# A graph network on one core: the last product taken in node order, and one-hot matrices and comparisons moved into one ring of seven buffers

## The chip, the cores and the metric

The kernel runs on one core of a Trainium2 chip. The time is device microseconds of one launch, the median of several runs: 3683.91 us over 12 runs, from 3669.29 to 3695.47.

The core has five engines, each with an instruction order of its own: PE multiplies matrices (PEld is its loading of weights), DVE (VectorE) and ACT (ScalarE) work on elements, POOL (GpSimd) issues here the gathers, and SP issues DMAs. They meet through semaphores.

## The reference

There are 16 graphs of N = 1024 nodes with C = 64 channels and a weighted adjacency matrix of 1024 x 1024 for each. Four layers follow one another, each of the form x = layernorm(x + f(x, adj)):

```
layer 0   f = adj @ (x @ W) + b
layer 1   neighbours with every second one or so removed ("dilated"), then per node and channel
          a weighted sum of three quantiles over the neighbours that are left, then an MLP
layer 2   h = x @ W_embed; three times h = relu(adj @ (h @ Wl + bl)); f = h @ W_proj + b_proj
layer 3   t = adj @ x; f = where(t > 0.5, 1, 0)
```

The last of them is the product that the change is about: t[node, channel] = sum over m of adj[node, m] * x[m, channel], compared with 0.5, added to x and normalised over the 64 channels of a node.

## The kernel before, in words

A graph is kept as T = 8 tiles of P = 128 nodes. Its adjacency is transposed once and stands in SBUF as `adjT[p, t, m, n]` (float32): the weight of the edge from node m * 128 + p to node t * 128 + n.

For each graph b three long pieces of work and some short ones are written as Python generators that emit a few instructions and yield a duration:

- `words_of` (L559): loads the adjacency row by row, transposes it on PE, compares it with zero on DVE into `nb` (L582 and L583, 1024 float16 per partition), packs the bits by a product with powers of two (L594), computes layer 0 and stores the transposed adjacency in DRAM (L590).
- `front` with `listing` (L613, L647): sorts the nodes by degree. DVE builds eight one-hot matrices `perm` (L717, one for each tile of 128 nodes), PE multiplies each with the packed words (L722 and L723, 16 instructions for each one), ACT copies the result out (L759 and L760), and DVE extracts from it the lists of neighbours (L768 to L793). A second one-hot, `back_to` (L621), is used once.
- `gathered`, `masked`, `quantiles`, `summed`: POOL gathers the neighbours' rows (L921), ACT masks them (L976), DVE sorts them by a network of minimum and maximum (L1026), ACT and PE sum the weighted rows (L1062, L1055).
- `back` (L1253): the rest of layer 1, layer 2 and layer 3. It begins in `to_nodes` (L1086), which brings the sums back from degree order to node order: the sums are split into three bfloat16 `pieces` (L1092); then for s = 0 to 7 ACT makes a one-hot `ones_at` in two instructions (L1105 and L1106) and PE multiplies it with the pieces (six instructions, L1110). It ends with layer 3: `aggregate` (L426) takes x3 as the weights of PE and streams the adjacency, 512 columns at a time, so that the product comes out as channels by nodes; ACT copies the two halves out of PSUM (L434); eight transposes (L1350) bring it into node order; DVE compares, adds (L1353) and normalises.

A float32 matmul stands in the trace as two records, each with a weight load of its own, so the 16 matmuls of L431 are 32 records.

The order of the instructions on every engine is fixed when the program is built. A heap holds the generators by a planned time; the earliest emits its next instructions and is put back later by what it yielded, times a stretch (178/181 for `back`, L1384). Planned time per graph is 192.06 units (`LENGTHS`); the `back` of a graph, the `front` of the next one and the `words_of` of the one after that run at the same time, with the quantiles of the groups between. So the eight `perm` and the eight `ones_at` fall into the same stretch. An engine runs what was emitted for it strictly in that order, so one instruction that waits holds up all that was emitted after it. Each gather on POOL is made to wait for the fifth last DVE and the fourth last ACT instruction emitted before it (`follow`, L899).

Buffers rotate by tag: the n-th allocation of a tag takes slot n modulo the number of slots, and who writes first into a slot waits until the readers of what stood there are done. Before, `nb`, `perm` (with `back_to`) and `ones_at` have a tag and two slots each. So `perm` number t waits until PE has read `perm` number t - 2, and `ones_at` number s until PE has read number s - 2.

The lines in `general` (L1151 on) are a fallback for graphs that do not fit the fixed sizes; no instruction of it stands in the trace.

Of the kernel before, what the change touches and what calls it, by code (L numbers as in the profile page):

```python
# [11 lines left out]
F16 = mybir.dt.float16  # L12
BF16 = mybir.dt.bfloat16
# [7 lines left out]
P = 128  # L21
# [185 lines left out]
def kernel(  # L207
# [36 lines left out]
    tmp = ctx.enter_context(tc.tile_pool(name="tmp", bufs=2))  # L244
# [7 lines left out]
    ident = const.tile([P, P], F32, name="ident")  # L252
# [170 lines left out]
            nc.scalar.copy(dst[:, h * HALF:(h + 1) * HALF], pt[:C, :])  # L423
            yield 1.0

    def aggregate(dst, adjT, src, bank):  # L426

        for h in range(NH):
            pa = bank()
            for m in range(T):  # L430
                nc.tensor.matmul(pa[:C, :], src[:, m, :], adjT[:, h * TH:(h + 1) * TH, m, :],  # L431
                                 start=(m == 0), stop=(m == T - 1))
                yield 1.3
            nc.scalar.copy(dst[:, h * HALF:(h + 1) * HALF], pa[:C, :])  # L434
            yield 0.7

    def layernorm(u, y, who, mean=False):

        def col(name):
# [119 lines left out]
    def words_of(st):  # L559


        b = st["b"]
        while b >= LIVES and "done" not in state[b - LIVES]:
            yield 0.5
        st["mb"] = mask_of(b)
        xt = load_x(b)
        hi = his[b % 2]
        lo = act.tile([P, T, W + 2], F16, tag="lo", name="lo", bufs=2)
        l0 = Layer0(xt)
        if b == 0:  # L570

            st["adjT"] = adjT = big.tile([P, T, T, P], F32, tag="adjB", name="adjB")
        else:
            st["adjd"] = adjd = dram.tile([P, T, T, P], F32, tag="adjd", name="adjd", bufs=LIVES)

        def block(t):
            if b == 0:
                return adjT[:, t]
            return big.tile([P, T, P], F32, tag="adjF", name="at", bufs=3)

        def words(t, a, at):
            nb = tmp.tile([P, T, P], F16, tag="nb", name="nb")  # L582
            vector.tensor_scalar(nb, at, 0.0, None, op0=ALU.is_gt)  # L583
            yield 0.3
            vector.tensor_tensor(nb[:, t, :], nb[:, t, :], off_diag, ALU.mult)
            if b:
                while "x1 is there" not in state[b - 1]:
                    yield 0.5
                yield from l0.feed(t, at)
                nc.scalar.dma_start(adjd[:, t], at)  # L590
            pw = psum_tp()
            for c in range(T):
                half = c // TH
                nc.tensor.matmul(pw[:, half * (W + 1):(half + 1) * (W + 1)], nb[:, c, :],  # L594
                                 pow2[:, c, :], start=(c % TH == 0), stop=(c % TH == TH - 1))
            yield 0.7
            nc.scalar.copy(hi[:, t, :W], pw[:, :W])
            nc.scalar.copy(lo[:, t, :], pw[:, W:2 * W + 2])
            yield 0.6

        yield from transposed(b, block, words)
        xc = act.tile([P, T, R], F32, tag="xc", name="xc", bufs=LIVES)
        st["x1"] = xc[:, :, :C]
        st["words"] = hi, lo, xc
        if b == 0:
            while "permuted" not in st:
                yield 0.5
            for t in range(T):
                yield from l0.feed(t, adjT[:, t])
        yield from l0.end(st["x1"])  # L610
        st["x1 is there"] = True

    def front(st):  # L613
        b = st["b"]
        while "words" not in st or (b >= 2 and ("all in", len(GROUPS) - 1) not in state[b - 2]):
            yield 0.5
        hi, lo, xc = st["words"]
        yield from listing(st, hi, lo)

        part, tile_of = st["home"]  # L620
        back_to = tmp.tile([P, T, P], F16, tag="perm", name="back_to")  # L621
        vector.tensor_tensor(back_to, iota[:, :P].unsqueeze(1).to_broadcast([P, T, P]),
                                spread(part, P), ALU.is_equal)
        yield 0.8
        in_tile = small.tile([P, T, T], F16, tag="in_tile", name="in_tile", bufs=1)
        vector.tensor_tensor(in_tile, iota[:, :T].unsqueeze(1).to_broadcast([P, T, T]),
                                spread(tile_of, T), ALU.is_equal)
        yield 0.6
        gone = small.tile([P, T, T, 2], F16, tag="gone8", name="gone8", bufs=1)
        vector.tensor_tensor(gone, in_tile.unsqueeze(3).to_broadcast([P, T, T, 2]),  # L630
                                st["gone"].unsqueeze(2).to_broadcast([P, T, T, 2]), ALU.mult)
# [12 lines left out]
        nc.scalar.dma_start(table[1:N + 1, :].rearrange("(t p) c -> p t c", p=P), xc)  # L644
        yield 3.0

    def listing(st, hi, lo):  # L647
# [5 lines left out]
        deg, do, h, odd = col("deg"), col("do"), col("h", I32), col("odd")  # L653
# [72 lines left out]
        if st["b"] == 0:  # L726

            rooms = [srt.tile([P, TH, N], F16, tag="x", name="perms", bufs=4) for _ in range(NH)]
            perms = [rooms[t // TH][:, t % TH, :] for t in range(T)]
            for t in range(T):  # L730
                one_hot(t, perms[t])
                yield 0.5
            halves = [range(h * TH, (h + 1) * TH) for h in range(NH)]
        else:
            for t in range(T):
                perm = tmp.tile([P, N], F16, tag="perm", name="perm")
                one_hot(t, perm)
# [348 lines left out]
    def to_nodes(dst, st):  # L1086
# [10 lines left out]
        st["moved"] = True  # L1097
        banks = [psum_mm() for _ in range(NH)]
        for s in range(T):
            ones_at = tmp.tile([P, N], BF16, tag="ones_at", name="ones_at", bufs=2)  # L1100
            if st["b"] == B - 1 and s % 3:
                vector.tensor_scalar(ones_at, iota, st["minus"][:, s:s + 1], 0.0,
                                        op0=ALU.add, op1=ALU.is_equal)
            else:
                nc.scalar.activation(ones_at, iota, AF.Abs, bias=st["minus"][:, s:s + 1])  # L1105
                nc.scalar.activation(ones_at, ones_at, AF.Relu, bias=1.0, scale=-1.0)  # L1106
            yield 1.9
            for h, bank in enumerate(banks):
                for i in range(S):
                    nc.tensor.matmul(bank[:C, :], pieces[:, i, s, :],  # L1110
                                     ones_at[:, h * HALF:(h + 1) * HALF],
                                     start=(s == 0 and i == 0), stop=False)
            yield 1.7
# [37 lines left out]
    def general(b):  # L1151
# [10 lines left out]
        def positions(t, a, at):  # L1162
            def col(name, dt=F32):
                return small.tile([P, 1], dt, tag="g" + name, name=name)

            nb = tmp.tile([P, N], F16, tag="nb", name="nb")
            vector.tensor_scalar(nb, a, 0.0, None, op0=ALU.is_gt)
            dg = nb[:, t * P:(t + 1) * P]
            vector.tensor_tensor(dg, dg, off_diag, ALU.mult)
            cum = tmp.tile([P, N], F16, tag="perm", name="cum")  # L1170
# [31 lines left out]
        nc.sync.dma_start(xrow, xT)  # L1202
        st["agg"] = act.tile([P, T, C], F32, tag="x3", name="agg")
        with tc.For_i(0, T, 1) as t:
            nb = tmp.tile([P, N], F16, tag="nb", name="nb")
# [3 lines left out]
            eT = tmp.tile([P, T, P], F16, tag="perm", name="eT")  # L1209
# [43 lines left out]
    def back(st):  # L1253
# [7 lines left out]
        adjT = st["adjT"]  # L1261
# [25 lines left out]
        def chan(name):  # L1287
            return act.tile([C, N], F32, tag="chan", name=name)
# [54 lines left out]
        x3 = node_tile("x3", "x3")  # L1343
        yield from residual(hT, wp_sb, 2 * C, x2, x3)

        tT = chan("tT")
        yield from aggregate(tT, adjT, x3, psum_mm)
        pt = psum_mm()
        for t in range(T):
            nc.tensor.transpose(pt[:, t * C:(t + 1) * C], tT[:, t * P:(t + 1) * P], ident[:C, :C])  # L1350
        yield 2.0
        u = wide_u("u3")
        vector.scalar_tensor_tensor(u, nodes(pt), 0.5, x3, op0=ALU.is_gt, op1=ALU.add)  # L1353
        yield 0.7
# [124 lines left out]
```

## Time and profile before

| | |
|---|---|
| median of 12 runs | 3683.91 us (3669.29 to 3695.47) |
| profiled execution, its own time | 3684.71 us |
| its span | 3682.8 us, so 1.9 us lie outside it |
| granted PE clock, mean | 0.814 |
| busy: PE, DVE, ACT, POOL | 72%, 76%, 52%, 59% |
| from the first `pieces` of one graph to that of the next | 216 us (596.1 to 3189.1 us holds twelve) |
| L431, the last product, PE | 264.4 us in 512 records |
| L1350, its transposes, PE | 16.7 us in 128 records |
| L434, its copies, ACT | 32 of about 0.578 us |
| L1105 and L1106, `ones_at` on ACT | 123 each, medians 1.134 and 1.057 us |
| L717, `perm` on DVE | 120, median 0.482 us |

No engine is busy all the time. In a program like this the sum of busy time says little; what counts in a stretch is the engine that the others wait for there, and the idle time that stands before an instruction on it. "remote" or "another core or an unknown queue" in an answer means that the instruction waited for a signal whose sender the profile cannot place. With one core there is no other core; it is in most cases a signal that came late.

### The profile page before, as it was taken

What the parts mean: (1) busy time and instruction counts of PE and PEld (TensorE: products, weight loads), DVE (VectorE), ACT (ScalarE), POOL (GpSimd) and SP (SyncE); (2) the same over time, 40 slices, a digit from 0 to 9 for tenths busy, and PEclk for the clock granted to TensorE, in tenths of its full rate; (3) what the DMA queues carried; (4) which work ended last, traced back from release to release, by engine and by line L of the source; (5) the groups of instructions that cost most, each with busy time, mean ns of one, the idle gap of its engine ahead of it and who ended that gap; (6) DMA issues with size and microseconds to landing.
All of it is one profiled execution on the core that took longest, in us unless ns stands there. A gap on an engine that the chain in (4) does not pass through costs nothing.

```text
span 3682.8 us, 49179 instructions
## 1 busy us (share of the span) xinstructions
PE 2665.1 (72%) x13765; PEld 1630.9 (44%) x13766; DVE 2797.7 (76%) x8020; ACT 1899.5 (52%) x6153; POOL 2171.0 (59%) x2078
## 2 busy tenths in 40 slices
PE   6334686867868686786868678686867868685678
PEld 5233453544445354454535444353544535342343
DVE  6287887968778796877879787786968778797650
ACT  2144555546464554646555564645556464555441
POOL 0666666566565656656665665656666665666600
PEclk8656797878879798887878888797888979777788
DMA  3232223323232332323233232323323232212110
GB/s 100 73 83 60 60 75 92 90 84 82 59 103 74 98 85 59 108 64 103 75 98 85 66 101 64 102 75 98 85 63 103 65 103 75 84 24 73 23 51 4
DMA packets 169079, 282.73 MB, mean 77 GB/s; under 512 B 99485, under 2 KB 102112, under 8 KB 166880
## 3 DMA queue, kind: packets, MB, share of 16 engines
q0 software_dynamic: 66048, 69.88, 11.6%
q1 hardware_dynamic: 67584, 142.01, 11.5%
q10 hardware_dynamic: 35168, 67.62, 4.9%
q8 instruction: 114, 1.87, 0.2%
q14 instruction: 165, 1.35, 0.1%
HBM read 204.33 MB, written 71.44 MB: 75 GB/s over the span
## 4 chain that ended last, share of the span: by engine, by line
DVE 32%; PE 31%; ACT 16%; another core or an unknown queue 14%; issue 5%; DMA 2%; DVEq 0%; ACTq 0%; POOL 0%; POOLq 0%
PE mm L1338 11%; DVE s L1026 8%; DVE g L1026 8%; ACT g L976 6%; PE ax L521 4%; DVE top L789 3%; PE mm L431 3%; ACT ones_at L1105 3%; PE mm L1110 2%; DVE cand L793 2%; ACT ones_at L1106 2%; ACT g L1062 2%; PE pa L1055 2%; PE tp L496 2%
## 5 line engine op out<-in xcount | busy, mean ns | idle before, releaser
L921 POOL DMA_INDIRECT g<-table,idx x1952 | 2048.0, 1049 | 1292.0 <-issue 336.7
L1338 PE MATMUL mm<-adjB,msg 128*128 128x512 f32 x1536 | 781.3, 631 | 41.6 <-issue 28.9
L1026 DVE TENSOR_TENSOR s<-g 128x384 f32<-128x384 f32 (+8 forms) x1200 | 576.3, 495 | 136.3 <-ACT g L976 94.9
L976 ACT ACTIVATE g<-g,bias 128x64 f32<-128x64 f32 (+9 forms) x2272 | 597.3, 339 | 87.3 <-DVE bias L972 71.7
L1026 DVE TENSOR_TENSOR g<-s 128x256 f32<-128x256 f32 (+10 forms) x1040 | 508.1, 500 | 8.8 <-remote 4.6
L1055 PE MATMUL pa<-g,ident 128*128 128x128 f32 (+1 forms) x1600 | 327.9, 333 | 132.4 <-ACT g L1062 80.4
L1062 ACT ACTIVATE g<-g,w 128x64 f32<-128x64 f32 x1552 | 393.0, 337 | 14.3 <-DVE w L1033 10.8
L1055 PEld LDWEIGHTS pa<-g,ident 128*128 128x128 f32 x1600 | 279.3, 230 | 269.9 <-issue 140.8
L1338 PEld LDWEIGHTS mm<-adjB,msg 128*128 128x128 f32 x1536 | 276.7, 200 | 263.8 <-issue 239.3
L1110 PE MATMUL mm<-ones_at,pieces 128*64 128x512 bf16 x768 | 246.0, 468 | 164.7 <-ACT ones_at L1106 128.0
L521 PE MATMUL ax<-at,xt 128*64 128x128 f32 x1920 | 306.1, 321 | 27.0 <-issue 26.6
L521 PEld LDWEIGHTS ax<-at,xt 128*64 128x64 f32 x1920 | 264.2, 164 | 90.0 <-issue 85.2
L431 PE MATMUL mm<-adjB,x 128*64 128x512 f32 x512 | 264.4, 647 | 14.6 <-issue 7.2
L1026 DVE TENSOR_TENSOR g<-g 128x256 f32<-128x256 f32 (+7 forms) x432 | 213.9, 505 | 4.4 <-remote 1.8
L1110 PEld LDWEIGHTS <-pieces 128*64 128x64 bf16 x768 | 95.4, 129 | 272.1 <-issue 229.3
L1026 DVE TENSOR_TENSOR g<-g,s 128x256 f32<-128x256 f32 (+5 forms) x512 | 209.1, 415 | 5.7 <-DVE at L674 1.3
L1341 ACT ACTIVATE hlT<-mm 128x512 f32<-128x512 f32 x96 | 57.3, 596 | 276.3 <-PE mm L1338 173.7
L722 PE MATMUL wd<-hi,perm 128*128 128x71 f16 x960 | 103.5, 223 | 126.6 <-DVE perm L717 94.6
L496 PE MATMUL tp<-ident,arow 128*128 128x128 f32 x1024 | 173.2, 300 | 29.6 <-DMA arow<-in_adj_dram 13.1
L1278 DVE TENSOR_TENSOR u<-mm,mb 128x512 f32<-128x512 f32 x32 | 22.1, 691 | 219.9 <-PE mm L1272 109.4
L498 ACT COPY at<-tp 128x512 f32<-128x512 f32 x240 | 138.0, 576 | 96.8 <-remote 55.1
L1105 ACT ACTIVATE ones_at<-iota,minus 128x1024 bf16<-128x1024 f16 x123 | 140.0, 1138 | 92.1 <-remote 47.2
(223 smaller groups left out, 4284.9 us busy)
## 6 DMA issues: line engine op xcount, KB each, us to landing
arow<-in_adj_dram SPq DMA_DIRECT2D x128, 512.0 KB
adjd<-at ACTq DMA_DIRECT2D x120, 512.0 KB
adjB<-adjd SPq DMA_DIRECT2D x15, 4096.0 KB
g<-table,idx POOLq DMA_INDIRECT x1952
table<-xc ACTq DMA_DIRECT2D x16, 264.0 KB
xt<-in_x_dram SPq DMA_DIRECT2D x16, 256.0 KB
out_dram<-y SPq DMA_DIRECT2D x16, 256.0 KB
stage<-table,packed POOLq DMA_INDIRECT x112
```

The lines of the kernel that those rows point to most:

```text
L431: nc.tensor.matmul(pa[:C, :], src[:, m, :], adjT[:, h * TH:(h + 1) * TH, m, :], start=(m == 0), stop=(m == T - 1))
L496: nc.tensor.transpose(pt[:, i * P:(i + 1) * P], a[:, j * P:(j + 1) * P], ident)
L498: nc.scalar.copy(at[:, h * TH:(h + 1) * TH, :], pt.rearrange("p (i n) -> p i n", n=P))
L521: nc.tensor.matmul(self.bank[:C, cols], self.xt[:, m + 1, :], at[:, m, :], start=(m == 0), stop=(m == T - 1))
L921: g = nc.gpsimd.indirect_dma_start(out=dst, out_offset=None, in_=st["table"], in_offset=bass.IndirectOffsetOnAxis(ap=index, axis=0))
L976: nc.scalar.activation(v, v, AF.Identity, bias=bias[:m, i, k:k + 1])
L1026: vector.tensor_tensor(box(bufs[mode >> 1 & 1], d, run, sd, count, tile), box(bufs[mode >> 3], a, run, sa, count, tile), box(bufs[mode >> ...
L1055: nc.tensor.matmul(pa[:, :(e - k) * nt * C], ident, rows_.rearrange("p (k c) -> p k c", c=R)[:, :, :C], start=(j == 0), stop=(j == len(run ...
L1062: nc.scalar.activation(slots(g, bufs[0], lo + r, lo + r + 1)[:, i, 0, :C], slots(g, bufs[at[r]], lo + r, lo + r + 1)[:, i, 0, :C], AF.Iden ...
L1105: nc.scalar.activation(ones_at, iota, AF.Abs, bias=st["minus"][:, s:s + 1])
L1110: nc.tensor.matmul(bank[:C, :], pieces[:, i, s, :], ones_at[:, h * HALF:(h + 1) * HALF], start=(s == 0 and i == 0), stop=False)
L1338: nc.tensor.matmul(pg, msg[:, m, :], adjT[:, h * TH:(h + 1) * TH, m, :], start=(m == 0), stop=(m == T - 1))
```

## The change

1. `aggregate`, its two copies and the eight transposes go. In their place, for each of the 8 node tiles, 8 matmuls take the 128 x 128 block `adjT[:, t, m, :]` as weights and stream the 64 columns of `x3[:, m, :]`, into 64 columns of one PSUM bank. The result is in node order at once. 64 matmuls (128 records with 128 weight loads) replace 16 (32 records) and the 8 transposes. They yield 1.4 after every four and 1.5 at the end: 23.9 planned units instead of 24.2.
2. `nb`, `back_to`, `perm` and `ones_at` share one tag, `onehot`, with seven slots of 2 KB per partition, instead of three tags with two slots each. In the fallback `nb`, `cum` and `eT` take the tag too.

```diff
-    def aggregate(dst, adjT, src, bank):
-
-        for h in range(NH):
-            pa = bank()
-            for m in range(T):
-                nc.tensor.matmul(pa[:C, :], src[:, m, :], adjT[:, h * TH:(h + 1) * TH, m, :],
-                                 start=(m == 0), stop=(m == T - 1))
-                yield 1.3
-            nc.scalar.copy(dst[:, h * HALF:(h + 1) * HALF], pa[:C, :])
-            yield 0.7
...
-            nb = tmp.tile([P, T, P], F16, tag="nb", name="nb")
+            nb = tmp.tile([P, T, P], F16, tag="onehot", name="nb", bufs=7)
...
-        back_to = tmp.tile([P, T, P], F16, tag="perm", name="back_to")
+        back_to = tmp.tile([P, T, P], F16, tag="onehot", name="back_to", bufs=7)
...
-                perm = tmp.tile([P, N], F16, tag="perm", name="perm")
+                perm = tmp.tile([P, N], F16, tag="onehot", name="perm", bufs=7)
...
-            ones_at = tmp.tile([P, N], BF16, tag="ones_at", name="ones_at", bufs=2)
+            ones_at = tmp.tile([P, N], BF16, tag="onehot", name="ones_at", bufs=7)
...
-        tT = chan("tT")
-        yield from aggregate(tT, adjT, x3, psum_mm)
         pt = psum_mm()
         for t in range(T):
-            nc.tensor.transpose(pt[:, t * C:(t + 1) * C], tT[:, t * P:(t + 1) * P], ident[:C, :C])
-        yield 2.0
+            for m in range(T):
+                nc.tensor.matmul(pt[:, t * C:(t + 1) * C], adjT[:, t, m, :], x3[:, m, :],
+                                 start=(m == 0), stop=(m == T - 1))
+                if m % 4 == 3:
+                    yield 1.4
+        yield 1.5
         u = wide_u("u3")
         vector.scalar_tensor_tensor(u, nodes(pt), 0.5, x3, op0=ALU.is_gt, op1=ALU.add)
```

More of the change, by code (lines that the diff above doesn't have):

```diff
@@ L1164, in col @@
                 return small.tile([P, 1], dt, tag="g" + name, name=name)
-            nb = tmp.tile([P, N], F16, tag="nb", name="nb")
+            nb = tmp.tile([P, N], F16, tag="onehot", name="nb", bufs=7)
             vector.tensor_scalar(nb, a, 0.0, None, op0=ALU.is_gt)
@@ L1169, in positions @@
             vector.tensor_tensor(dg, dg, off_diag, ALU.mult)
-            cum = tmp.tile([P, N], F16, tag="perm", name="cum")
+            cum = tmp.tile([P, N], F16, tag="onehot", name="cum", bufs=7)
             vector.tensor_tensor_scan(cum, nb, nb, 0.0, op0=ALU.add, op1=ALU.max)
@@ L1204, in general @@
         with tc.For_i(0, T, 1) as t:
-            nb = tmp.tile([P, N], F16, tag="nb", name="nb")
+            nb = tmp.tile([P, N], F16, tag="onehot", name="nb", bufs=7)
             nc.sync.dma_start(nb, keys[ds(t * P, P), :])
@@ L1208, in general @@
             nc.sync.dma_start(e, removed[ds(t * P, P), :])
-            eT = tmp.tile([P, T, P], F16, tag="perm", name="eT")
+            eT = tmp.tile([P, T, P], F16, tag="onehot", name="eT", bufs=7)
             nc.sync.dma_start(eT, removed[:, ds(t * P, P)].rearrange("(m p) n -> p m n", p=P))
```

## The prediction

> **What bounds the kernel now.** I read the page first: the busy shares and the chain that ended last. No engine is full, and the chain is spread over three of them, so the time is made of waits between engines and has to be read stage by stage.
>
> ```profile
> PE 2665.1 (72%) x13765; PEld 1630.9 (44%) x13766; DVE 2797.7 (76%) x8020; ACT 1899.5 (52%) x6153; POOL 2171.0 (59%) x2078
> ...
> DVE 32%; PE 31%; ACT 16%; another core or an unknown queue 14%; issue 5%; DMA 2%; DVEq 0%; ACTq 0%; POOL 0%; POOLq 0%
> ...
> L431 PE MATMUL mm<-adjB,x 128*64 128x512 f32 x512 | 264.4, 647 | 14.6 <-issue 7.2 <-DVE x L468 6.5 <-DMA stage<-table,packed 0.6
> L1110 PE MATMUL mm<-ones_at,pieces 128*64 128x512 bf16 x768 | 246.0, 468 | 164.7 <-ACT ones_at L1106 128.0 <-issue 36.5
> ```
>
> The reader is to see that PE waits 128 us for the one-hots of ACT, and that 14% of the chain is late signals.
>
> Second, the lines L1105 (`ones_at` on ACT) and L717 (`perm` on DVE): how long the engine sat idle ahead of them, and what ended it. The instructions need nothing of PE but a free buffer, so a release by PE's L1110 or L723 is the wait for a slot. "remote" I count as the same wait with a late signal.
>
> ```profile
> L1105 ACT ACTIVATE ones_at<-iota,minus x123: 1131/1134/1150, 381.3 to 3573.8; 128x1024 bf16<-128x1024 f16 x123
> ...
>   remote: 47.2, 12
>   PE mm L1110: 37.5, 11
>   PE wd L723: 7.1, 4
> ```
>
> ```profile
> L717 DVE TENSOR_SCALAR perm<-iota,rank x120: 473/482/702, 170.3 to 3210.5; 128x1024 f16<-128x1024 f16 x120
> ...
>   remote: 17.7, 6
>   PE mm L1110: 17.0, 5
>   PE wd L723: 8.8, 7
> ```
>
> So 91.8 us of ACT and 43.5 us of DVE are spent waiting for slots. Third, the list of waits by place: who is late after that, and what stands at the last product.
>
> ```profile
> DVE u L1353 <- PE mm L1350: 66.7, 11, 17.1
> DVE cand L768 <- ACT wd L759: 66.5, 14, 14.0
> ```
>
> Fourth, one stretch of the last product, all engines: PE is busy 22.60 of 22.60 us and ACT 10.19. PE bounds it. Last, the chain in order of time at the end of the program, where one graph is alone and durations are clean.
>
> ```profile
> 2288.40:2311.00 22.60, 22.60 (x77) 8.62 (x76) 13.82 (x63) 10.19 (x37) 16.04 (x17) 0.91 0.18 31
> ```
>
> ```profile
> 3633.19 13.73 PE mm L1338 x32
> ...
> 3647.25 1.94 PE mm L1272 x16
> ...
> 3653.96 15.90 PE mm L431 x32
> 3669.89 0.59 ACT tT L434
> 3670.48 0.04 issue
> 3670.52 0.47 PE mm L1350 x4
> 3671.02 0.70 DVE u L1353
> ```
>
> **The product in node order.** L1272 has the shape of the new matmuls: weights 128 x 128, 64 columns streamed, float32. At full clock 16 records take 1.94 us, of which the last one alone is 0.278 us (its mean in that stretch), so records start every (1.94 - 0.278) / 15 = 0.111 us. 128 of them are 14.2 us. The old 32 records at full clock go by L1338, also 512 columns: 13.73 us. In the middle of the run L431 took (264.4 - 15.9) / 15 = 16.6 us, 1.21 times that, from the slower clock and from the work of others between. With the same factor the new product takes 17.2 us. The transposes, 16.7 / 16 = 1.0 us, go. PE: +0.6 - 1.0 = -0.4 us per graph. The bounds: 14.2 us, if the factor falls away (-3.4), and L542, the same shape in the same stretch but in runs of four to eight records, 41.3 us for 256, 0.161 each, 20.6 us (+3.0). I take -0.4: the new records come in groups of eight and more, nearer to the run of 16 than to those.
>
> The Trainium skill, "TensorE: Matmul & The Clock Gate", section "LDWEIGHTS (loading the stationary operand)", speaks against this part: a weight load costs its columns divided by 1.2 GHz, about 107 ns for 128, however little is streamed after it, and here each load serves 64 columns. By the page's figure alone 128 loads are an estimated 13.7 us at full clock, where the 0.111 us of the trace give 14.2, and the sum would be the same; if stream and load did not overlap it would be more, which the row of L1272 does not show.
>
> ACT loses two copies of 0.578 us. It is 10.19 us busy of 22.60 there, so this is worth nothing by itself. But the last copy and the transposes lie between the product's end and DVE's L1353: 1.1 us in the clean end (3669.89 to 3671.02). In twelve of the other 15 graphs it is 4 to 6.5 us, as the product's signal comes late to ACT. Against it: the last four matmuls are now emitted 1.4 + 1.5 = 2.9 units ahead of L1353, the last one was 1.3 + 0.7 + 2.0 = 4.0 ahead; 1.1 units are 1.2 us, and others have a quarter of PE there (5.5 of 22.6 us), so 0.3 us more is in front of the product's end. At L1353: 0.4 + 1.1 - 0.3 = 1.2 us earlier. DVE waits there 66.7 - 17.1 (the end) = 49.6 us in 15 graphs, 3.3 each, so it can use it. Since a late signal costs the same whoever waits, I count half, 0.6 us, 9 us in all. Ends: 3.3 x 15 = 50 us gained, and 45 us lost with the +3.0.
>
> PSUM: the product takes one bank instead of two and one more; the bank's last reader is DVE's L1278, a layer norm earlier: nothing. No DMA is added, removed or moved on SP, ACT's queue or POOL. The gathers that follow the fourth last ACT instruction point, near the two lost copies, to one or two instructions earlier and may start up to 1 us sooner; POOL is 16.04 of 22.60 us busy there and nobody waits for these rows until the masks of a later group, so nothing.
>
> **The ring of seven.** Per graph 25 tiles pass it: eight each of `nb`, `perm`, `ones_at`, and `back_to`. While `perm` and `ones_at` alternate, a slot was last used three or four of each kind ago, not two. The waits of 91.8 us (ACT) and 43.5 us (DVE) go nearly whole; what stood behind them moves up: on ACT the masks L976 and the copies L759 and L760, on DVE the sort steps, and for DVE the next late thing is L768, which waits for L759 and this for PE's last L723 and for ACT's order.
>
> How early can L768 be? From the first `pieces` to L768 ACT has 4.5 us for the pieces, 8 x (1.13 + 1.06) = 17.5 us of one-hots, 5.8 us of masks between (24 of about 0.24 in the graph at 1682 us) and about 1.5 us to L768: 29.3. In the fourteen graphs with both it took 33.9 us in the mean, between 30.6 and 40.5. So 0 to 4.6 us per graph. I take 2.6, somewhat over half: the signals of PE that came late for a slot can come late for L759, the wait that comes next. 14 x 2.6 = 36 us (0 to 64). Work after L768 is on DVE, which is in the chain from there for 50 us on end (the chain from 1519 to 1570 us is DVE throughout), so a gain there is kept.
>
> `nb` gets nothing: L583 never waited for PE (its idle time was ended by ACT's L498). `back_to` neither. If the ring made one of them wait, it would be for a reader seven allocations back, at least 10 us earlier at the measured pace of 216 us for 25. An ACT writer in a slot that DVE wrote may need one more semaphore instruction, 0.02 us each, 16 x 25 = at most 8 us over all engines, in gaps: nothing.
>
> **The end.** The last graph is alone. Its one-hots: ACT waits 8.2 us for slots and PE 8.3 us for one-hots; two of the three rows of ACT in that chain (2 x 2.2 us) lie on it. With free slots ACT makes its three and DVE its five ahead of PE; PE has 48 records of 0.229 us, some at half clock, about 12.9 us from 3563.4 to 3576.3 instead of 3578.8: -2.5. The product: 14.2 + 0.2 + the 2.2 us that the old one lost to the cold clock (15.90 - 13.73) = 16.6 against 17.1: -0.5. Together -3 us.
>
> Sum: -9 - 36 - 3 = -48 us. The profiled execution was 3684.7 us, 0.8 over the median; I predict 3640 us, a little less than the whole sum (-44), 1.2% faster. Its own range is 3600 to 3676.
>
> **The rivals.** (1) *The small matmuls are dear among the others* (slower). For: L1272 has in the whole run 100.1 us in 512 records, 0.196 each, and PE sat idle 51.1 us at them with nothing to wait for, where L431 with as many records has 7.2. Against: these gaps are all at the rows with `wp_sb`, after the long stall of each period, and L542 does not have them. Between 0.161 and 0.196, at 0.178, the product is 22.8 us, 5.2 over the old 17.6; 15 x 5.2 = 78, less the 39 of ring and end: 3724. It decides from where the loss passes 2.6 us per graph: 20.2 us, 0.158 us per record.
>
> (2) *The wait moves.* For: 14% of the chain is late signals, and at 2796 us L759 itself waited 6.4 us. PE's signal is late while POOL issues gathers one after the other, and POOL stops when DVE and ACT stop; with slots free they stop first at L759. Then only the end and a little remain, -3 to -10 us: 3678.
>
> (3) *All of it is kept*: 64 + 1.2 x 15 + 3 = 85 us: 3600.
>
> (4) *POOL runs on longer and signals come later everywhere*: against it, that POOL is busy 59% and its gathers are not more. One more stall of 5 us per graph, set against the gain: 3685 + 75 - 48 = 3712.
>
> **How the numbers follow.** Forecast 0.56, (1) 0.13, (2) 0.14, (3) 0.11, (4) 0.06. A median of runs that spread by 0.7% can tell about 0.2% (7.4 us) from no change. Faster: the forecast but for 0.02, all of (3), half of (2): 0.72. Same: the other half of (2) and a little of the forecast: 0.09. Slower: (1) and (4): 0.19. The range 3592 to 3690 leaves out (1) and (4) and takes in the rest.
>
> **What would show it.** Right: no idle time at L1105 and L717 that ends with PE; L768 about 31 us after the first `pieces`; a product of 16 to 18 us of PE per graph at 0.12 to 0.135 us per record; DVE's wait at L1353 smaller by about 1 us per graph; a period of about 213 us instead of 216. Wrong: the wait at L768 for L759 grown to 8 us or more (2); the product at 20 us or more, with idle "issue" between its records (1); more "remote" in all (4). What would make it wrong besides: a shifted order of DVE, since the emission times after the product move by 0.3 units, which I count as nothing.

## The result: 3.9% slower

The changed kernel takes 3829.34 us in the median of 11 runs, against 3686.09 us for the kernel before (46 runs by now). The ratio is 1.0391, 95% interval 1.0374 to 1.0407. The forecast was 3640 us with a range of 3592 to 3690. The profiled execution has a span of 3824.4 us, 141.6 more than before.

In the changed kernel L1094 and L1095 make `ones_at`, L706 makes `perm`, L748 and L757 are the copy and the sort step that follow it (L759 and L768 before), L1327 is layer 2's product (L1338 before). L1338 is now the last product and L1344 the comparison that reads it.

From the page of the changed kernel, the chain that ended last and two of its groups (busy us, mean ns of one, idle us ahead of them):

```profile
PE 44%; DVE 23%; ACT 14%; another core or an unknown queue 11%; issue 6%; DMA 1%; ACTq 0%; DVEq 0%; POOL 0%; POOLq 0%
...
L1338 PE MATMUL mm<-x,adjB 128*128 128x64 f32 x2048 | 427.2, 392 | 53.2 <-issue 47.5
...
L1099 PE MATMUL mm<-ones_at,pieces 128*64 128x512 bf16 x768 | 242.6, 457 | 102.6 <-ACT ones_at L1095 55.2
```

PE went from 31% of the chain to 44%. The product takes 427.2 / 16 = 26.7 us per graph, where the old one with its transposes took 17.6. These 9.1 us in sixteen graphs are 146 us: the size of the whole loss. That the sizes agree does not show that it is one cause; the experiments below find two. PE's wait for one-hots fell from 128.0 to 55.2 us, so the ring does something, too. The idle time ahead of `ones_at` (L1094) and of `perm` (L706), and the two waits that the prediction showed:

```profile
L1094 ACT ACTIVATE ones_at<-iota,minus x123: 1131/1133/1150, 389.2 to 3698.4; 128x1024 bf16<-128x1024 f16 x123
...
  remote: 16.9, 6
  PE mm L1099: 12.1, 2
```

```profile
L706 DVE TENSOR_SCALAR perm<-iota,rank x120: 474/481/616, 167.4 to 3318.9; 128x1024 f16<-128x1024 f16 x120
...
  remote: 26.3, 4
  PE mm L1099: 11.1, 2
```

```profile
DVE u L1344 <- PE mm L1338: 132.5, 16, 27.7
...
DVE cand L757 <- ACT wd L748: 104.2, 16, 15.3
```

ACT's waits for slots are 29.0 us (16.9 + 12.1) instead of 91.8. DVE's are 37.4 instead of 43.5. But DVE waits 104.2 us for the copy L748, where it was 66.5: the first sort step stands 35.4 us after the first `pieces` (twelve graphs), and stood 34.2 us after it before. The wait of DVE at the product doubled, from 66.7 to 132.5 us. The period of a graph is 224.1 us instead of 216.1.

The end of the program is clean of all this. The chain of the changed kernel in order of time (start, us), and PE's clock in the same stretch (the two columns after the engines' busy times are the granted clock and the DMA share):

```profile
3764.36 13.73 PE mm L1327 x32
...
3778.41 1.94 PE mm L1261 x16
...
3785.13 27.59 PE mm L1338 x128
3812.74 0.70 DVE u L1344
```

```profile
3764.40:3778.00 13.60, 13.60 (x32) 5.70 (x30) 0.00 (x0) 1.18 (x2) 0.00 (x0) 1.00 0.00 1
...
3785.20:3789.00 3.80, 3.80 (x18) 3.80 (x19) 0.00 (x0) 0.00 (x0) 0.00 (x0) 0.50 0.00 0
...
3805.00:3812.70 7.70, 7.70 (x37) 7.52 (x36) 0.00 (x0) 0.00 (x0) 0.00 (x0) 0.50 0.02 4
```

The shape of L1261 is that of the product, and its 16 records still take 1.94 us. But PE is busy in every part of these 27.6 us and its clock does not rise from 0.50. The old product ran here at 0.88 in the mean: it started cold and was at full speed after about 4 us. In the start times of the records, 1527 of 1941 distances within the product, over all graphs, are 0.20 to 0.25 us, twice the 0.111 us that the prediction used; 312 are at 0.10 to 0.13 us. In ten of the sixteen graphs the clock stands at 1.00 when the product begins and falls to 0.50 between 2.1 and 4.7 us later; in all sixteen it is then at 0.50 until the last 2 to 3 us of the product, or until its end.

### The profile page after: what moved, and what is told of

It is laid out like the page before. It is cut to its first block, busy times and chain, and to the rows that moved or that the text cites. A ratio compares the mean times of both kernels' runs of the same rounds, so it can differ in the third digit from the quotient of the medians.

```text
span 3824.4 us, 51968 instructions
## 1 busy us (share of the span) xinstructions
PE 2850.0 (75%) x15173; PEld 1991.3 (52%) x15174; DVE 2796.7 (73%) x8020; ACT 1882.3 (49%) x6121; POOL 2169.8 (57%) x2078
## 4 chain that ended last, share of the span: by engine, by line
PE 44%; DVE 23%; ACT 14%; another core or an unknown queue 11%; issue 6%; DMA 1%; ACTq 0%; DVEq 0%; POOL 0%; POOLq 0%
PE mm L1327 12%; PE mm L1338 11%; DVE s L1015 6%; DVE g L1015 5%; PE ax L510 5%; ACT g L965 5%; ACT ones_at L1094 3%; PE pa L1044 3%; PE mm L1316 2%; ACT g L1051 2%; ACT ones_at L1095 2%; PE mm L1099 2%; PE tp L485 2%; DVE top L778 2%
## 5 line engine op out<-in xcount | busy, mean ns | idle before, releaser
L1327 PE MATMUL mm<-adjB,msg 128*128 128x512 f32 x1536 | 787.5, 633 | 37.3 <-issue 28.8
L1338 PE MATMUL mm<-x,adjB 128*128 128x64 f32 x2048 | 427.2, 392 | 53.2 <-issue 47.5
L1338 PEld LDWEIGHTS mm<-x,adjB 128*128 128x128 f32 x2048 | 417.4, 308 | 58.9 <-issue 50.9
L1327 PEld LDWEIGHTS mm<-adjB,msg 128*128 128x128 f32 x1536 | 277.8, 202 | 268.2 <-issue 248.6
L1099 PE MATMUL mm<-ones_at,pieces 128*64 128x512 bf16 x768 | 242.6, 457 | 102.6 <-ACT ones_at L1095 55.2
L711 PE MATMUL wd<-hi,perm 128*128 128x71 f16 x960 | 111.8, 223 | 144.1 <-DVE perm L706 85.1
L1099 PEld LDWEIGHTS <-pieces 128*64 128x64 bf16 x768 | 91.5, 125 | 214.5 <-issue 166.3
L711 PEld LDWEIGHTS <-perm 128*128 128x128 f16 x960 | 87.5, 117 | 186.6 <-DVE perm L706 94.9
L443 DVE TENSOR_REDUCE ln_v<-sq 128x8 f32<-128x512 f32 x64 | 43.7, 682 | 190.7 <-ACT sq L440 188.0
```

Source lines behind the costliest of these rows:

```text
L711: nc.tensor.matmul(pw[:, :hn], ws, hi[:, t, :], start=False, stop=False)
L1099: nc.tensor.matmul(bank[:C, :], pieces[:, i, s, :], ones_at[:, h * HALF:(h + 1) * HALF], start=(s == 0 and i == 0), stop=False)
L1327: nc.tensor.matmul(pg, msg[:, m, :], adjT[:, h * TH:(h + 1) * TH, m, :], start=(m == 0), stop=(m == T - 1))
L1338: nc.tensor.matmul(pt[:, t * C:(t + 1) * C], adjT[:, t, m, :], x3[:, m, :], start=(m == 0), stop=(m == T - 1))
```

## The experiments

Each ratio is against the kernel before on the same chip. The runs came to five chips, and these are of two kinds: on three the kernel before takes 3721 to 3732 us, on two 3171 to 3176 us. On the first kind PE's signals come late, as in the profile before; on the second, waits put down to "remote" are absent. I call them chips with and without late signals. Each chip was used on one occasion only, so whether the chip itself or something else on that occasion makes the difference was not shown. The first comparison (3686 us) was of the kind with them.

### The two parts alone, and the product with twice the columns (a chip with late signals, 3721.5 us)

`e1_ring` keeps the ring and takes the old product; `e2_product` keeps the product and takes the old tags with two slots. `e3_wide` is the whole change, `e4_wide_alone` the product without the ring. Both stream x3 twice, into two banks, and DVE reads the first 64 of each 128 columns. The matmul, against the product alone:

```diff
-        pt = psum_mm()
+        pts = [psum_mm() for _ in range(NH)]
         for t in range(T):
+            pt = pts[t // TH][:, (t % TH) * 2 * C:(t % TH + 1) * 2 * C]
             for m in range(T):
-                nc.tensor.matmul(pt[:, t * C:(t + 1) * C], adjT[:, t, m, :], x3[:, m, :],
+                nc.tensor.matmul(pt, adjT[:, t, m, :],
+                                 x3[:, m, :].unsqueeze(1).to_broadcast([P, 2, C]),
...
```

> The ring of seven alone, the product as before. Theory A (the loss is the product's: its 128 records of 64 columns keep the granted PE clock at 0.50, 27.6 us where 14.4 were expected): the product's extra PE time, 427.2 - 264.4 - 16.7 = 146 us, is the whole loss of 143, so the ring alone is worth nothing net: 3670 to 3690 us. ACT's waits for slots fall from 92 to about 30 us as after the change, and the wait at DVE's first cand (L757) stays near 75 to 90 us. Theory B (the ring is at fault: with free slots POOL's gathers run on and PE's signals come late at the copies L748): the ring alone costs 50 us or more, 3730 to 3830. My forecast's step for it: 3640 to 3650.

> The product in node order alone, the three old tags with two slots. Theory A: 3800 to 3850 us, product at 0.20 to 0.214 us per record in every graph and clock 0.50 while it runs alone at the end. Theory B: 3690 to 3740, the rest of the 143 us coming from the ring.

> The change with each matmul of the product streaming 128 columns, x3 twice, into two banks, of which DVE reads one half: twice the streaming, the same 128 weight loads, one DVE instruction more. Theory A (the clock follows how much is streamed, not whether PE is occupied): at the end the clock rises to 1.00 after some 4 us and 128 records take 15 to 18 us instead of 27.6; in the middle 0.12 to 0.15 us per record; the run 3660 to 3700. Rival C (the clock stays low because of the weight loads or of the float32 form itself, 128 loads without a pause): 27.6 us or more at the end, the run 3820 to 3900. Rival D (128 blocks of weights read from the adjacency are slow in themselves, by SBUF): 27 us or more too, with the clock at 1.00.

> The product with 128 columns streamed and the old tags, no ring. Theory A: 3660 to 3690 us. Against e3 it shows once more what the ring is worth: if e3 is lower by more than 10 us the ring helps when the product does not hide it, if it is higher the ring costs.

| | us | ratio | 95% interval |
|---|---|---|---|
| ring alone | 3720.5 | 1.0011 | 0.9989 to 1.0033 |
| product alone | 3859.8 | 1.0370 | 1.0332 to 1.0407 |
| ring and product, 128 columns | 3801.1 | 1.0205 | 1.0163 to 1.0248 |
| product alone, 128 columns | 3779.9 | 1.0167 | 1.0112 to 1.0223 |

The loss is the product's, and the ring is worth nothing. Theory B is out. With 128 columns the median with the ring is 21 us above the one without, but four runs of each spread over 25 and 34 us, so that this is not clear of noise. In the ring alone, the idle time ahead of L1105, that ahead of L717, DVE's wait at the sort step, and ACT's waits at the copy L759, last as they are in the kernel before:

```profile
L1105 ACT ACTIVATE ones_at<-iota,minus x123: 1131/1133/1150, 387.9 to 3585.2; 128x1024 bf16<-128x1024 f16 x123
...
  PE mm L1110: 24.2, 6
  remote: 20.8, 9
```

```profile
L717 DVE TENSOR_SCALAR perm<-iota,rank x120: 475/482/685, 172.8 to 3237.6; 128x1024 f16<-128x1024 f16 x120
...
  PE mm L1110: 25.2, 5
  remote: 19.5, 7
```

```profile
DVE cand L768 <- ACT wd L759: 67.1, 15, 8.4
...
ACT wd L759 <- remote: 52.2, 11, 15.5
...
ACT wd L759 <- PE wd L723: 40.8, 6, 12.6
```

```profile
ACT wd L759 <- remote: 22.0, 9, 8.9
...
ACT wd L759 <- PE wd L723: 12.8, 1, 12.8
```

ACT's waits for slots halve (91.8 to 45.0 us), DVE's do not fall at all (44.7 in these two lines), and the sort step comes 35.8 us after the first `pieces`, 1.6 later than before. ACT gained 46.8 us at the slots and lost 58.2 at L759, the next place where it needs PE: 93.0 us instead of 34.8.

With 128 columns streamed the clock opens (rises from 0.50 to 1.00). The product in the last graph of `e4_wide_alone`, in three stretches:

```profile
3739.20:3743.20 4.00, 4.00 (x19) 4.00 (x20) 0.00 (x0) 0.00 (x0) 0.00 (x0) 0.50 0.01 2
3743.20:3747.20 4.00, 4.00 (x34) 4.00 (x34) 0.00 (x0) 0.00 (x0) 0.00 (x0) 0.90 0.00 0
3747.20:3756.00 8.80, 8.80 (x79) 8.62 (x78) 0.42 (x1) 0.00 (x0) 0.00 (x0) 1.00 0.02 4
```

Twice the streaming takes 16.8 us instead of 27.6. So the low clock is not made by the weight loads, of which there are as many, nor by the reading of the adjacency: rivals C and D fall. Nor does it matter that the wide product has two banks: the clock is at 1.00 from 4.8 us on, after some 23 records, and the first 64 write into one bank. The difference is worth 1.0370 - 1.0167 = 2.0% here. But theory A forecast a run at the level of the kernel before, and 1.7% are left.

### How many columns, and single tags with three slots (a chip without late signals, 3171.4 us)

`e5_cols96` streams 96 columns, 64 that are needed and 32 that DVE does not read; `e6_cols32` streams 32 and leaves out the other half of the channels; both are without the ring. `e7_ones3` and `e8_perm3` are the kernel before with three slots in one tag:

```diff
-            ones_at = tmp.tile([P, N], BF16, tag="ones_at", name="ones_at", bufs=2)
+            ones_at = tmp.tile([P, N], BF16, tag="ones_at", name="ones_at", bufs=3)
...
-                perm = tmp.tile([P, N], F16, tag="perm", name="perm")
+                perm = tmp.tile([P, N], F16, tag="perm", name="perm", bufs=3)
```

> The product alone in node order (old tags), each matmul streaming 96 columns (a node tile and half of the next, of which DVE reads the first 64), two banks. At full clock a record is bound by its weight load, 0.111 us, of which 96 columns are streamed for 0.080; at 64 it was half of the time, at 128 nearly all. If the clock is set by the streamed share of the time (theory A) the question is on which side of it 96 falls: rising, 16 to 18 us for the product of the last graph; staying at 0.50, 27.6. Rival C (the clock follows the weight loads) gives 27.6 here as with 64.

> The product alone in node order with 32 columns streamed: the second half of the 64 channels is left out of the comparison, so the result is not the reference's. Theory A: half the streaming changes nothing, since a record at half clock is bound by its weight load: 27 to 27.7 us for the last graph at 0.50, the run within 0.5% of the product alone (ratio 1.03 to 1.04). If the cost lay in what is streamed or written to PSUM it would fall to some 14 to 20 us.

> The kernel before with three slots for ones_at instead of two and nothing else. If the ring of seven gained nothing because perm and ones_at wait for one another in it, three slots of its own give ACT what was forecast: waits for slots from 92 to under 45 us, DVE's first cand 1 to 2 us earlier per graph, 3655 to 3675 by the time of the first comparison (ratio 0.992 to 0.998). If it gained nothing because the late signal of PE comes at the next wait instead, the waits for slots fall, those at L759 grow and the ratio is 0.998 to 1.004.

> The kernel before with three slots for perm and back_to instead of two and nothing else. First cause (coupling in the ring): DVE's waits before perm from 44 to under 20 us, ratio 0.994 to 0.999. Second (the late signal comes at the next wait): ratio 0.998 to 1.004, the wait at the first cand larger by what the perm lines lost.

The last product at the end of the program, with 96 and then with 32 columns:

```profile
3133.90:3137.90 4.00, 4.00 (x19) 4.00 (x19) 0.00 (x0) 0.00 (x0) 0.00 (x0) 0.50 0.00 0
3137.90:3141.90 4.00, 4.00 (x34) 4.00 (x33) 0.00 (x0) 0.00 (x0) 0.00 (x0) 0.88 0.00 0
3141.90:3150.80 8.90, 8.87 (x80) 8.70 (x78) 0.42 (x1) 0.00 (x0) 0.00 (x0) 1.00 0.01 4
```

```profile
3286.20:3290.20 4.00, 4.00 (x19) 4.00 (x20) 0.00 (x0) 0.00 (x0) 0.00 (x0) 0.50 0.01 2
3290.20:3313.70 23.50, 23.50 (x111) 23.36 (x110) 0.00 (x0) 0.00 (x0) 0.00 (x0) 0.50 0.01 1
```

96 columns open the clock as 128 do; 32 do not, and take the same 27.5 us as 64, so neither the streaming nor the writing into PSUM is what costs. At full clock 512 columns take 0.429 us, 0.84 ns a column. Of the 0.111 us of a record 32 columns fill 24%, 64 fill 48%, 96 fill 72%. What opens the clock lies between the last two, though PE is busy without a gap in all of them. As a record is 0.111 us long in all four, its streamed share and its number of columns cannot be told apart here. The ratios are 0.9965 (0.9952 to 0.9977) with 96 columns and 1.0499 (1.0478 to 1.0520) with 32, more than the 1.03 to 1.04 that I expected: in all thirteen graphs ahead of the last three the clock stands at 1.00 when the product begins, and with 32 columns it falls to 0.50 within 0.9 to 5.9 us, where with 96 it stays up in all thirteen.

The two kernels with three slots, 0.9994 (0.9984 to 1.0003) and 1.0000 (0.9990 to 1.0009), tell nothing of the ring: on this chip hardly any wait for a slot is left to win. ACT waits 8.0 us for `ones_at` slots with two of them and 4.7 with three, DVE 0.5 us for `perm` with either. Whether single tags would gain on a chip with late signals was not tried.

### The gathers taken away from POOL (another chip with late signals, 3731.9 us)

```diff
-            g = nc.gpsimd.indirect_dma_start(
-                out=dst, out_offset=None, in_=st["table"],
-                in_offset=bass.IndirectOffsetOnAxis(ap=index, axis=0))
+            gathered.n = getattr(gathered, "n", 0) + 1
+            r0 = 1 + (gathered.n * 61) % (N - P)
+            g = nc.sync.dma_start(dst, st["table"][r0:r0 + P, :])
             follow(g)
...
+    vector.tensor_scalar(total, total, 0.0, None, op0=ALU.mult)
```

The rows are the wrong ones, and the last line keeps the kernel out of its fallback.

> The kernel before with every gather of POOL replaced by a plain DMA of 128 rows of the same table on SP's queue, with the same two waits for DVE and ACT: the indices are left out, so the result is not the reference's. Theory P (PE's signals come late while POOL issues gathers one after the other): "remote" and the share of the chain that no engine explains fall from 14% to a few per cent, the waits for slots from 135 us to under 30, and the run is 5 to 12% faster. If the signals are late for another reason (DMA traffic, the profile), they stay.

> The product in node order, old tags, and the gathers on SP as in the run beside it, indices left out again. Cold clock: the product stays at 0.20 to 0.214 us per record without POOL too, and costs 8 to 11 us per graph against the run beside it, if PE bounds that stretch. The gaps of 1.2 to 2.1 us between its records (47.5 us "issue" in all after the change) go if POOL makes them.

> The ring of seven with the old product and the gathers on SP, indices left out. If the ring's gain was eaten by late signals at the next wait, then without them it is seen, if there is any wait for a slot left: 0 to 1% faster than the run with the gathers on SP alone. If the waits for slots are gone there without the ring, the two are the same within 0.3%.

The old kernel with the gathers on SP takes 3109.7 us, ratio 0.8329 (0.8277 to 0.8380), which is more than the 5 to 12% that I expected. Its chain, where no wait of unknown origin is left:

```profile
DVE 41%; PE 38%; ACT 15%; DMA 3%; issue 2%; SPq 1%; ACTq 0%; DVEq 0%
```

The list of its waits has no "remote"; ACT waits 7.0 us for slots. With the ring it waits none and takes 3104.7 us (0.8315): the same. So theory P holds: the late signals, and with them nearly all of the waits that the ring was to remove, come with POOL's gathers; by what path was not shown. Seventeen per cent of this kernel's time on such a chip goes there. A DMA with no indices is less work than a gather, and how much of the 17% that is the run cannot say; on the chips without late signals, where the gathers run on POOL, the kernel takes 3171 to 3176 us, about 2% more, and if a gather's own work is the same on both kinds, that bounds it.

The product of 64 columns with the gathers on SP takes 3164.4 us, 0.8475 (0.8339 to 0.8611), 55 more than its neighbour. No distance between its records exceeds 0.95 us, where 29 of them in the changed kernel add up to 43.3 us. And its clock has two states: in six of the first thirteen graphs the product runs at 0.112 us per record and takes 19 us; in the other seven most records are at 0.213 and it takes 32, and in the last three all are, in 27.6 to 28.0. In these seven graphs, too, the clock stands at 1.00 when the product begins; it falls 1.6 us later.

### The change, and 96 columns, on a chip without late signals (3176.1 us)

`e13_cols96_ring` is the change with 96 columns, `e14_cols96` the kernel of `e5_cols96`, `e15_change` the change, `e12_sp_wide` the kernel of `e4_wide_alone` with the gathers on SP.

> The product with 128 columns, old tags, gathers on SP as before (indices left out). If the rest of the loss needs POOL's late signals, this is 3095 to 3115 us, at or up to 0.5% under the old product with the gathers on SP (3109.7), with no gap over 0.95 us between its records (they had 41.5 us with POOL). If the product of 128 records is dear by itself, 3130 to 3170.

> The whole change with 96 columns streamed instead of 64. On a chip with late signals (3680 to 3730 us before) ratio 1.010 to 1.022, as with 128 columns; on one without (3170) 0.994 to 0.998.

> The product with 96 columns and the old tags, as in e5, on this chip. With late signals ratio 1.010 to 1.020; without 0.995 to 0.998. Within 0.4% of e13, since the ring is worth nothing.

> The change itself on this chip. With late signals ratio 1.037 to 1.041. Without, only the cold clock is left: 13 graphs of about 10 us and the end, some 140 us of 3170, less where the clock stays up: 1.025 to 1.05.

| | us | ratio | 95% interval |
|---|---|---|---|
| product of 128 columns, gathers on SP | 3075.4 | 0.9682 | 0.9649 to 0.9715 |
| ring and product, 96 columns | 3156.3 | 0.9942 | 0.9921 to 0.9963 |
| product alone, 96 columns | 3159.6 | 0.9949 | 0.9930 to 0.9968 |
| the change, 64 columns | 3201.2 | 1.0071 | 1.0044 to 1.0098 |

The first row lies 0.9 to 1.1% under the old product with the gathers on SP (3104 to 3110 us on two other chips), more than the 0.5% that I expected at most. With the clock held up the product in node order is a gain of half a per cent here; with 64 columns it is a loss of 0.7%, not the 2.5% or more that I expected, as the clock stays up in ten of the first thirteen graphs. Two products of the change on this chip, then a third one in three stretches, the product's records alone (busy us of PE and of its weight loads, the clock, DMA share, GB/s):

```profile
1220.40:1239.30 18.90, 15.44 (x128) 14.92 (x128) 1.00 0.18 29
1585.50:1618.80 33.30, 26.26 (x128) 25.75 (x128) 0.55 0.18 28
```

```profile
661.60:663.40 1.80, 1.78 (x16) 1.78 (x16) 1.00 0.10 19
663.50:690.70 27.20, 20.00 (x90) 19.70 (x89) 0.50 0.19 29
690.80:693.50 2.70, 2.70 (x24) 2.58 (x23) 1.00 0.18 31
```

The same instructions, 15.44 or 26.26 us. The state in which the product begins does not decide alone: the third one begins at 1.00, falls after 1.8 us and is back 27 us later. What the runs show is that at 64 columns a clock that is up can stay up or fall, and that one that has fallen comes back late: with gathers and late signals a stretch at 0.50 lasts 31 to 65 us in the first thirteen graphs of the change, and 3.4 to 13.7 us in those of `e4_wide_alone`, with 128 columns. Whether 64 columns by themselves hold a clock up for long was not shown: in the graphs where it stays up, 41 other instructions of PE stand between the 128 records, and at most 40 records, 4.3 us, follow one another alone. What makes it fall in one graph and not in the next is open. In the change's first profile, on a chip with late signals, it was at 0.50 for most of the product in all sixteen graphs.

### What is left on a chip with late signals (3723.5 us)

`e16_short` is the kernel before with the old product, its weights, copies and transposes, cut into shorter matmuls; the planned units, and with them the order of what is emitted elsewhere, stay as they were. `e17_wide_again` is `e4_wide_alone`, `e18_sp_again` is `e9_sp`.

```diff
-            for m in range(T):
-                nc.tensor.matmul(pa[:C, :], src[:, m, :], adjT[:, h * TH:(h + 1) * TH, m, :],
-                                 start=(m == 0), stop=(m == T - 1))
-                yield 1.3
+            for i in range(TH):
+                for m in range(T):
+                    nc.tensor.matmul(pa[:C, i * P:(i + 1) * P], src[:, m, :], adjT[:, h * TH + i, m, :],
+                                     start=(m == 0), stop=(m == T - 1))
+                    if m % 4 == 3:
+                        yield 1.3
```

> The kernel before with the product's 16 matmuls of 512 columns cut into 64 of 128 (128 records, weights x3 of 64 columns loaded for each), all else as before. If many short records are dear where POOL's gathers hold PE up, then on a chip with late signals ratio 1.008 to 1.020, with gaps over 0.95 us between the records; on one without, 0.997 to 1.003 and no such gaps. If the number of records is harmless, 0.997 to 1.003 on both.

> The product with 128 columns, old tags, again. With late signals ratio 1.012 to 1.022 as in the first run of it; without, 0.993 to 0.998, as with 96 columns.

> The old kernel with the gathers on SP (indices left out), on this chip. If the kind of chip matters only through POOL's gathers, 3095 to 3125 us here too, whatever the kernel before takes on it: ratio 0.83 on a chip with late signals, 0.975 to 0.985 on one without.

The short records alone make it 3806.3 us, 1.0224 (1.0179 to 1.0270), a little over the 1.008 to 1.020 that I expected. The product of 128 columns is 1.0197 (1.0145 to 1.0250) here, not to be told from it. In a graph in the middle and in the last graph, the records of the short product:

```profile
2360.70:2396.00 35.30, 20.83 (x128) 18.41 (x128) 0.79 0.12 20
3774.20:3790.30 16.10, 16.07 (x128) 15.86 (x128) 0.88 0.00 1
```

And its line in the list of groups, over the whole run:

```profile
L432 PE MATMUL mm<-adjB,x 128*64 128x128 f32 x2048 | 310.1, 314 | 42.2 <-issue 36.3 <-DVE x L470 5.7
```

In the last graph, where POOL is done, 128 short records take 16.1 us, where 32 long ones took 15.9. Among the gathers the stretch is 35 us long, where the prediction's window of the same product showed 22.60; in the thirteen graphs with gathers it is 31 to 38 us, with long records 21 to 29. 25 distances over 0.95 us add up to 37.4 us (4 and 5.5 us with long records), and the clock falls to half in between: 452 of 1946 distances are at 0.20 to 0.25 us. In the whole run PE is busy 310.1 us with the product instead of 264.4 and sits idle 42.2 us ahead of its records instead of 14.6. Of PE's extra time at the product, then, slower records are more (45.7 us, with equal speed in the last graph) than idle time (27.6 us). So where signals come late, cutting a product into four times as many records costs 2% by itself. The kernel with gathers on SP is 3104.4 us, 0.8334, as on the other such chip, which is what was expected if the kind of chip matters only through POOL's gathers.

On a chip with late signals, then, the change's 3.9% are about 2% that any product of 128 records loses there, in gaps and in the clock that falls with them, about 2% more because with 64 columns the clock does not come back, and nothing for the ring. The split is an estimate from `e2_product` and `e4_wide_alone`, which ran on one chip. Why PE issues short records so haltingly there is open: the long ones may give it time to get ahead, but that was not shown.

## Why the prediction was wrong, point by point

- **The product's PE time.** This step failed: "128 of them are 14.2 us", times 1.21 for the middle of the run, 17.2 us. It measured 26.7 us. The distance of 0.111 us was right for 16 records that follow 32 long ones at a clock of 1.00, and nothing in that row says how the clock does when such records go on for long. I took the clock of the stretch as a property of the stretch; the runs with 32 to 128 columns show that it depends on what PE streams. PE's idle time between the records, 7.2 us with the old product, was left as it was and came to 47.5. The factor 1.21, from long records, carried that mistake along. The row that was nearest in kind, L542 at 0.161 us among the gathers, was put aside for the wrong reason, that longer runs would do better.
- **The rule of the Trainium skill** on weight loads ("TensorE: Matmul & The Clock Gate", "LDWEIGHTS (loading the stationary operand)") gave 13.7 us for the loads, and at full clock the trace agrees (0.111 us a record). The rule names no clock; "at full clock" is the prediction's reading. At half clock the record takes 0.213 us, which the rule does not cover. The same page's Part 1, on the clock gate, says that about 3.4 us of sustained matmul activity release the clock. These runs come near it for 96 columns and more (in the last graph half clock for 4.0 to 5.3 us, then 1.00), and differ for 64 and 32: some 27.5 us of matmuls without a gap at 0.50. The measurement decides: here matmuls that stream 48% of a record's time did not release the clock, and matmuls that stream 72% did.
- **L1353 earlier by 1.2 us, half of it counted.** It came later: DVE's wait there went from 66.7 to 132.5 us. The copy and the transposes are gone as forecast, and the product's end moved by more.
- **The ring, 36 us.** Failed, as the second rival said: the waits for slots fell (ACT by 62.8 us), and the same lateness showed at the next wait for PE, L757 behind L748, 104.2 instead of 66.5 us; with the ring alone it showed at ACT's copy L759, 93.0 instead of 34.8 us. The argument that this wait would take less than half was without a row. The runs with the gathers on SP show why: without the late signals there are hardly any waits for slots to win (7.0 us), and with them a free slot only moves the place where they are met. The working had a slip as well: the mean of 33.9 us is that of thirteen graphs; with the first one it is 34.4.
- **The end, -3 us.** Half right: from the first `pieces` to the last L1099 the last graph takes 18.4 us instead of 21.0, -2.6 against the -2.5 forecast. The product there is 27.6 us instead of the 16.6 forecast.
- **Costed at nothing.** ACT's two copies, the bank and the fewer units cannot be told apart from the rest; the ring's unchanged total bounds those of the ring. A shifted order of DVE is not needed for the loss of a product in 128 records: `e16_short`, which shifts nothing, loses as much as `e17_wide_again`.
- **The rivals.** The first one is what happened, with a threshold of 0.158 us per record and 0.209 measured, and the outcome 3829 us lies over its price of 3724, as it stopped at 0.178 and held only the issue of short records against them, not the clock. The second is what happened to the ring. The fourth did not: "remote" was not more after the change (669 us in the sum of all listed waits, 702 before). The range left out the first rival, which I held for 13%; with two rows of the same shape at 0.161 and 0.196 against one at 0.111 it deserved far more.

## What to carry to other kernels

Before turning a product so that weights change with every 64 columns, work out which share of each record is streaming: at 72% the clock opened, at 48% a clock that had fallen was down for 27 us and more, and streaming the same columns twice made the product faster. A row of a few short matmuls right after long ones gives their price at the clock of the long ones. And where a signal comes late for a reason that stays, more buffers move the wait to the next place where the signal is needed; find out first what makes it late.

## What the runs showed of the hardware that I had not expected

- PE's granted clock follows how much each record streams, not whether PE is occupied: in the last graph 128 records without a gap stay at 0.50 for some 27.5 us with 32 or 64 columns, and are at 1.00 after 4.0 to 5.3 us with 96 or 128. On a chip without late signals it stayed up through all of the first thirteen products with 96 columns and through none with 32; with 64 through ten: 15.44 us at 1.00 and 26.26 us at 0.55 in one execution.
- Chips, or the occasions on which they were used, differ by 17% in the same kernel, 3171 to 3176 against 3721 to 3732 us, and on the slower kind the difference goes away when POOL issues no gathers (3104 to 3110 us). On the quicker kind no wait stands as "remote" in the profiles.
- On the slower kind a product of 128 short records costs 2% more than the same one in 32 long records, among gathers only.
- No kernel with the reference's result beats the kernel before on both kinds of chip: the change with 96 columns is 0.6% faster than the kernel before on the quicker kind of chip, and the product of 128 columns is 1.7 to 2.0% slower on the other. 96 columns were not run there.
